# Score products of 128 query rows at a time in a cross-attention kernel with layer norm

## The chip, the cores and the metric

The kernel runs on one core of one Trainium2 chip. The metric is the device time of one execution in microseconds. Engines are named as in the profile: PE is the matmul engine and PEld its weight loads, DVE, ACT and POOL the vector, scalar and GpSimd engines, SP the engine that issues most of the DMAs.

## The reference, cut to what matters

Four batches of 2048 query rows of 512 numbers attend to 77 context rows each; there are 16 heads of 32 numbers. All data is float32. The result is added to the input and layer-normalised.

```
qs = (x @ wq) as 16 heads of 32          # x: (4, 2048, 512)
ks, vs = (ctx @ wk), (ctx @ wv)          # ctx: (4, 77, 512), as 16 heads of 32
scores = einsum('bhqd,bhkd->bhqk', qs, ks) / sqrt(32)
scores = where(mask, -inf, scores)       # (4, 16, 2048, 77)
attn   = einsum('bhqk,bhkd->bhqd', softmax(scores), vs)
out    = attn @ wo + x
result = (out - mean) / sqrt(var + 1e-5) * gamma + beta
```

## The kernel before

The 8192 query rows are 64 tiles of 128 rows. Query projections (`q_visit`, tiles `pq`) are made for groups of 512 rows; the output projection (`o_proj`, tiles `po`) and the scores are made by tile. Both projections run as three products of float32 parts split into a high and a low half (`wqh`/`wql`, `xth`/`xtl`, `woh`/`wol`, `AH`/`AL`), each with 128x128 weights. The scores and the products of attention with values (`av`, tiles `pa`) are plain float32 products.

`qd[t // 4]` holds the projected queries with the head dimension on the partitions: four heads stand one below the other, 32 partitions each, and `g` numbers the four such sets. `kct` holds the keys in the same way. So a score product `score(t, g, j, ...)` uses the 32 rows of the array at `HD * j`, has the queries of head `(g, j)` as its weights and streams the 77 columns of the keys. The four `j` use the four row groups of the array, and their results go to four PSUM banks (one bank per `j`, tiles `sc`), query rows on the partitions.

`scores` serves one tile. `scores_pair` and `scores_rest` serve two tiles `2b` and `2b + 1` together: 32 units of a head and a tile, eight for each `j`, six of them in the bank of their own (`sc_b_0` to `sc_b_3`) and two in a bank that two `j` share (`sc_b_e` and `sc_b_f`). For even `j` the units in the shared bank come first, for odd `j` last.

DVE then takes each head's scores with the mask and writes negated masked scores to `pbuf` and their minima to `nm` (`maxima`, one instruction for 128 rows of one head), ACT makes the exponentials and their sums (`exps`), DVE the reciprocals, POOL the division (`normalise`), DVE transposes in blocks (`transp`), SP's DMAs regroup the blocks into `PT`, and `av` multiplies by the values. ACT and DVE split the result into `AH` and `AL`; `o_proj`, the residual sum and the layer norm follow.

The order of all work is written by hand. Six tiles run in a loop of their own, with `scores`. Then `pair(n)` walks the words of `PAIR` for n = 3 to 26, two tiles each; a word such as `T1.30` is one step (`S` is `scores_pair`, `D` is `scores_rest`, `T` is `maxima`, `e` is `exps`, `Q` is `q_visit`, `O` is `o_proj`, `V` is `av`). `ORDER` then names the steps for the rest, with `S54` to `S63` as `scores` of one tile. On PE the sequence of a pair is: `av`, the scores of `S` and `D`, two output projections, two query projections.

Of the kernel before, what the change touches and what calls it, by code (L numbers as in the profile page):

```python
# [17 lines left out]
P = 128  # L18
# [8 lines left out]
GH = 4  # L27
# [49 lines left out]
def xattn_layernorm(  # L77
# [29 lines left out]
    def bank(name):  # L107
        while len(ring) % 8 in kept:
            ring.append(ring[-8])
        ring.append(ring[-8] if kept else ps.tile([P, 512], F32, tag="mm", name=name))  # L110
        return ring[-1]
# [49 lines left out]
    def keys_of(h):  # L161
        return slice(TAIL_K, NK2) if h % 2 == 0 else slice(0, NK)

    fx, gx, qd, qp, bat, pts = {}, {}, {}, {}, {}, {}
    scs, nmax, sums, bts, at, pas = {}, {}, {}, {}, {}, {}
# [142 lines left out]
    def scores(t):  # L308
        nmax[t] = sb.tile([P, H], F32, tag="nm", bufs=3, name=f"nm_{t}")
        sums[t] = sb.tile([P, H], F32, tag="sum", bufs=3, name=f"sum_{t}")  # L310
        sc = [bank(f"sc_{t}_{j}") for j in range(GH)]
        scs[t] = {(g, j): sc[j][:, g * NK : (g + 1) * NK] for g in range(NG) for j in range(GH)}
        for g in range(NG):
            for half in range(0, P, P // 2):
                for j in range(GH):
                    score(t, g, j, half, P // 2)

    def score(t, g, j, r0, n):
        q = slice(HD * j, HD * (j + 1))
        at = (t % 4) * P + r0  # L320
        nc.tensor.matmul(  # L321
            scs[t][g, j][r0 : r0 + n],
            qd[t // 4][q, g, at : at + n],
            kct[q, g, t // TPB, keys_of(j)],
            start=True,
            stop=True,
        )

    def scores_pair(b):
        for t in (2 * b, 2 * b + 1):  # L330
            nmax[t] = sb.tile([P, H], F32, tag="nm", bufs=3, name=f"nm_{t}")
            sums[t] = sb.tile([P, H], F32, tag="sum", bufs=3, name=f"sum_{t}")
            scs[t] = {}
        own = [bank(f"sc_{b}_{j}") for j in range(GH)]
        both = [bank(f"sc_{b}_{j}") for j in ("e", "f")]
        units = []
        for j in range(GH):
            mine = [(2 * b, g) for g in range(NG)] + [(2 * b + 1, g) for g in range(NG)]
            for i, (t, g) in enumerate(mine):
                bk, at = (own[j], i) if i < 6 else (both[j // 2], 2 * (j % 2) + i - 6)  # L340
                scs[t][g, j] = bk[:, at * NK : (at + 1) * NK]
            units.append(mine[6:] + mine[:6] if j % 2 == 0 else mine)
        for i in range(6):
            for half in range(0, P, P // 2):
                for j in range(GH):
                    score(*units[j][i], j, half, P // 2)
        held[b] = units

    def scores_rest(b):
        units = held.pop(b)  # L350
        for i in (6, 7):
            for js in ((0, 2), (3, 1)):
                for half in range(0, P, P // 2):
                    for j in js:
                        score(*units[j][i], j, half, P // 2)

    def maxima(t, lo, hi):
        pb = pbuf[t % NPB]
# [410 lines left out]
    for u in range(0, JOIN, 2):  # L769
        n = u // 2  # L770
# [5 lines left out]
        for t in (u - 4, u - 3):  # L776
            if t >= 0:
                load_x(t)
        scores(u)
        maxima(u, 0, H // 2)  # L780
        if u == 2:
# [53 lines left out]
        if u >= 4:  # L835
            av(n - 2)
            av_hi(n - 2, 0)
            av_hi(n - 2, 1)
        scores(u + 1)
        maxima(u + 1, 0, H // 4)  # L840
        if u >= 4:
# [42 lines left out]

    tile_ops = {
        "S": scores, "r": recip, "n": normalise, "t": transp, "W": av_tile, "x": load_x, "O": o_proj,
        "X": lambda t: resid(t, range(NC_D // 2 if t == NT - 1 else NC_D)), "+": residual, "u": rsqrt_one, "y": centre, "z": finish, "k": scale, "f": affine, "w": store,
        "v": bias_one, "K": stretch, "G": shift, "p": pool_scale, "I": act_mean, "J": act_squares, "M": keep,
# [48 lines left out]
    def pair(n):  # L937
        u = 2 * n
        words = PAIR.split()
        if n == JOIN // 2:  # L940
            words.remove("O-6")
            words.insert(words.index("D"), "O-6")
        for word in words:
            op, k, part, queue = read(word)
            if op == "S":
                scores_pair(n)
            elif op == "D":
                scores_rest(n)
            elif op in "LB":
                m, at = divmod(u, TPB)  # L950
                if m + 1 < NB and op == "L" and at == TPB - 10:
                    load_mask(m + 1)
                elif m + 1 < NB and op == "B" and at >= TPB - 8:
                    mask_quarter(m + 1, (at - TPB + 8) // 2)
            elif op == "P" and "." not in word:
                regroup(n + k)
            elif op in "Qq":
                if op == "Q" or divmod(2 * n + k, 4) in qp:
                    do(op, 2 * n + k)
            elif op in "gij":  # L960
                do(op, n + k)
            elif op in "PVab":
                if op in "PV" or n + k > JOIN // 2 - 3:
                    do(op, n + k, part, queue)
            elif u + k >= 0:
                do(op, u + k, part, queue)
# [54 lines left out]
```

## Time and profile before

| what | value |
|---|---|
| time, median of 3 runs | 506.53 us (506.32 to 507.22) |
| the profiled execution | 508.02 us, span 506.2 us |
| PE busy | 497.0 us, 98% of the span |
| ACT busy | 473.0 us, 93% |
| DVE busy | 463.0 us, 91% |
| POOL busy | 427.6 us, 84% |
| mean granted PE clock | 0.997 |

The times are of whole executions; the span is the time from the first to the last instruction of the profiled one. Rows of groups give line, engine, operation, output and inputs, the part of the array (rows*columns), shapes and count, then busy time and mean nanoseconds of one, then idle time before it and what ended it. In rows of a timeline the first number is the start and the second the length, both in microseconds. The chain that ended last is followed back from the last instruction, from each piece of work to what released it. A float32 product that is not split by the kernel shows in the trace as two weight loads and two matmuls.

### The profile page before, as it was taken

Reading aid. Unit: us, or ns where it says so; the run is one execution under the profiler, and the core shown is the slowest. Engines: PE = TensorE matmul, PEld = TensorE weight load, DVE = VectorE, ACT = ScalarE, POOL = GpSimd, SP = SyncE. Lnnn points to the kernel's source line nnn. Section 1 sums busy time; section 2 is a strip of 40 time slices with the busy share of each in tenths; the row PEclk is TensorE's granted clock in tenths of the full one; section 3 lists DMA queues with packets and bytes.
Section 4 is the critical chain, followed back from the end, with each engine's and each line's share of the span. In section 5 each row is a group of like instructions: output and inputs, shape, how many; then the busy total and the mean of one; then the engine's idle time right before and its main releaser. Section 6 shows DMA issues by size and latency. Waiting matters only on the chain.

```text
span 506.2 us, 20441 instructions
## 1 busy us (share of the span) xinstructions
PE 497.0 (98%) x6908; PEld 391.7 (77%) x6908; DVE 463.0 (91%) x2567; ACT 473.0 (93%) x2240; POOL 427.6 (84%) x384
## 2 busy tenths in 40 slices
PE   9999999999999999999999999999999999999995
PEld 7987678777777877777787777778777777777784
DVE  6698899999989988999998998999999889999997
ACT  6798899999999999999999999999999999999971
POOL 0559367989988988989998888999988888999995
PEclk9999999999999999999999999999999999999998
DMA  8945867677887778878777877877778787677665
GB/s 314 388 168 149 222 187 194 190 196 202 231 229 218 223 201 219 229 209 229 213 219 211 232 199 223 229 224 227 216 196 221 199 247 235 170 189 222 167 210 208
DMA packets 58280, 109.50 MB, mean 216 GB/s; under 512 B 9203, under 2 KB 10739, under 8 KB 58176
## 3 DMA queue, kind: packets, MB, share of 16 engines
q1 hardware_dynamic: 55776, 103.35, 71.7%
q0 software_dynamic: 1872, 4.20, 2.8%
q8 instruction: 55, 0.90, 0.8%
q10 hardware_dynamic: 528, 0.66, 0.4%
q14 instruction: 49, 0.40, 0.3%
HBM read 41.68 MB, written 16.78 MB: 115 GB/s over the span
## 4 chain that ended last, share of the span: by engine, by line
PE 79%; DVE 8%; ACT 7%; DMA 2%; issue 1%; SPq 1%; POOL 0%; POOLq 0%; DVEq 0%; ACTq 0%
PE pq L192 27%; PE po L564 26%; PE pa L459 10%; ACT pbuf L379 7%; PE sc L321 6%; DVE B L413 2%; PE sc L564 2%; DVE pbuf L364 2%; PE sc_e L321 2%; PE pk L218 1%; PE pq L725 1%; PE pq L190 1%; PE sc_f L321 1%; SPq L425 1%; DMA out<-o 1%
## 5 line engine op out<-in xcount | busy, mean ns | idle before, releaser
L379 ACT ACTIVATE pbuf<-pbuf,nm 128x77 f32<-128x77 f32 x1024 | 352.6, 349 | 8.6 <-DVE nm L364 7.8
L379 ACT ACTIVATION_READ_ACCUMULATOR pbuf<-pbuf,nm 128x1 f32 x1024 | 193.9, 189 | 0.0
L390 POOL TENSOR_TENSOR pbuf<-pbuf,ri 128x1232 f32<-128x1232 f32 x63 | 145.9, 2316 | 20.8 <-DVE ri L385 17.4
L364 DVE CUSTOM_DVE_ANT_0 pbuf<-sc,mb 128x77 f32<-128x77 f32 x828 | 143.9, 231 | 6.9 <-PE sc L321 6.4
L192 PE MATMUL pq<-xtl,wqh 128*128 128x512 f32 (+1 forms) x256 | 98.3, 384 | 0.0
L192 PE MATMUL pq<-xth,wql 128*128 128x512 f32 (+1 forms) x256 | 98.2, 384 | 0.0
L413 DVE STREAM_TRANSPOSE B<-pbuf 128x1280 f32<-128x1280 f32 x63 | 94.6, 1503 | 0.4
L564 PE MATMUL po<-woh,AH 128*128 128x512 f32 x224 | 90.7, 405 | 0.0
L192 PE MATMUL pq<-xth,wqh 128*128 128x512 f32 (+1 forms) x230 | 88.6, 385 | 0.0
L564 PE MATMUL po<-wol,AH 128*128 128x512 f32 x224 | 87.3, 390 | 0.0
L592 POOL TENSOR_TENSOR o<-o,gam 128x512 f32<-128x512 f32 x53 | 68.7, 1295 | 21.5 <-ACT o L588 21.5
L564 PE MATMUL po<-woh,AL 128*128 128x512 f32 x224 | 86.5, 391 | 0.0
L364 DVE DVE_READ_ACCUMULATOR2_ANT nm<- 128x1 f32 x1024 | 84.4, 82 | 0.0
L593 POOL TENSOR_TENSOR o<-o,bet 128x512 f32<-128x512 f32 x53 | 68.3, 1289 | 4.2
L180 POOL TENSOR_TENSOR xtl<-xtf,xth 128x1024 fp32r<-128x1024 f32 x28 | 67.4, 2409 | 0.1
L459 PE MATMUL pa<-PT,vsb 96*32 96x256 f32 x960 | 58.2, 382 | 1.6 <-DVE vsb L267 1.0
L321 PE MATMUL sc<-kct,q 32*64 32x77 f32 x3312 | 56.0, 238 | 0.5 <-DVE q L209 0.5
L192 PEld LDWEIGHTS pq<-xth,wql 128*128 128x128 f32 x256 | 48.2, 188 | 8.4
L192 PEld LDWEIGHTS pq<-xtl,wqh 128*128 128x128 f32 x256 | 48.1, 188 | 8.4
L321 PEld LDWEIGHTS sc<-kct,q 32*64 32x64 f32 x3312 | 49.3, 130 | 6.5 <-issue 4.4
L564 PEld LDWEIGHTS po<-woh,AH 128*128 128x128 f32 x224 | 42.0, 188 | 10.7 <-DVE nm L364 0.4
L192 PEld LDWEIGHTS pq<-xth,wqh 128*128 128x128 f32 x230 | 43.2, 188 | 9.0
(191 smaller groups left out, 855.1 us busy)
## 6 DMA issues: line engine op xcount, KB each, us to landing
PT<-B SPq DMA_DIRECT2D x355, 128.0 KB
xtf<-xT SPq DMA_DIRECT2D x28, 512.0 KB
o<-x SPq DMA_DIRECT2D x56, 256.0 KB
out<-o SPq DMA_DIRECT2D x56, 256.0 KB
PT<-B POOLq DMA_DIRECT2D x16, 128.0 KB, 4.5
o_end<-x SPq DMA_DIRECT2D x7, 256.0 KB
out<-o_end SPq DMA_DIRECT2D x7, 256.0 KB
xtf<-xT SPq DMA_DIRECT2D x4, 256.0 KB
```

The costliest lines, as they stand in the source:

```text
L180: nc.gpsimd.tensor_tensor(l, fx.pop((g, c)), h.bitcast(F32), ALU.subtract)
L190: nc.tensor.matmul(pq[:, cols], wc, r[:, c, cols], start=False, stop=False)
L192: nc.tensor.matmul(pq, wc, r[:, c, rs], start=(n == 0), stop=(n == 11))
L321: nc.tensor.matmul(scs[t][g, j][r0 : r0 + n], qd[t // 4][q, g, at : at + n], kct[q, g, t // TPB, keys_of(j)], start=True, stop=True,)
L364: nc.vector.tensor_tensor_reduce(pb[:, i // 2, (i % 2) * NK : (i % 2 + 1) * NK], scs[t][g, j], mb[:, t % TPB, keys_of(h)], -1.0, CEIL, ALU ...
L379: nc.scalar.activation(p, p, AF.Exp, bias=nmax[t][:, i : i + 1], scale=-1.0, accum_out=sums[t][:, i : i + 1])
L390: nc.gpsimd.tensor_tensor(pv, pv, rv.to_broadcast((P, NP, 2, NK)), ALU.mult)
L413: nc.vector.transpose(bt.rearrange("p c q r -> p q c r"), pbuf[t % NPB].rearrange("p q (c r) -> p q c r", c=5),)
L459: nc.tensor.matmul(pas[b, g // 2][HD * j : HD * (j + 1), (g % 2) * BLK : (g % 2 + 1) * BLK], vsb[:, 2 * b // TPB, HD * h : HD * (h + 1)], ...
L564: nc.tensor.matmul(pos[t], a[:, c, rs], w[:, c], start=(first and n == 0), stop=(n == 11))
L592: nc.gpsimd.tensor_tensor(o, o, gam, ALU.mult)
L593: nc.gpsimd.tensor_tensor(o, o, bet, ALU.add)
```

## The change

A score product takes all 128 query rows of its tile as weights, so it uses 32 rows and all 128 columns of the array, where it took 64 rows of the tile and 64 columns. One product replaces two. Nothing else is edited; the banks, the heads' order and the hand-written order stay as they are.

```diff
         for g in range(NG):
-            for half in range(0, P, P // 2):
-                for j in range(GH):
-                    score(t, g, j, half, P // 2)
-
-    def score(t, g, j, r0, n):
+            for j in range(GH):
+                score(t, g, j)
+
+    def score(t, g, j):
         q = slice(HD * j, HD * (j + 1))
-        at = (t % 4) * P + r0
+        at = (t % 4) * P
         nc.tensor.matmul(
-            scs[t][g, j][r0 : r0 + n],
-            qd[t // 4][q, g, at : at + n],
+            scs[t][g, j],
+            qd[t // 4][q, g, at : at + P],
             kct[q, g, t // TPB, keys_of(j)],
...
         for i in range(6):
-            for half in range(0, P, P // 2):
-                for j in range(GH):
-                    score(*units[j][i], j, half, P // 2)
+            for j in range(GH):
+                score(*units[j][i], j)
...
         for i in (6, 7):
             for js in ((0, 2), (3, 1)):
-                for half in range(0, P, P // 2):
-                    for j in js:
-                        score(*units[j][i], j, half, P // 2)
+                for j in js:
+                    score(*units[j][i], j)
```

On PE, the start of a pair's scores (n = 4; `sc_e`, `sc_1`, `sc_f` and `sc_3` are the banks of `j` = 0 to 3 there). Before, the first two units of each `j`:

```order
L321 MATMUL sc_e<-kct,q_907 64x77 [waits DVE_49,PE_49]
L321 MATMUL sc_1_1335<-kct,q_907 64x77 [waits DVE_49]
L321 MATMUL sc_f<-kct,q_907 64x77 [waits DVE_49]
L321 MATMUL sc_3_1337<-kct,q_907 64x77 [waits DVE_49,PE_49]
L321 MATMUL sc_e<-kct,q_907 64x77
L321 MATMUL sc_1_1335<-kct,q_907 64x77
L321 MATMUL sc_f<-kct,q_907 64x77
L321 MATMUL sc_3_1337<-kct,q_907 64x77
L321 MATMUL sc_e<-kct,q_907 64x77 [waits DVE_49]
```

and now:

```order
L320 MATMUL sc_e<-kct,q_827 128x77 [waits DVE_49]
L320 MATMUL sc_1_1207<-kct,q_827 128x77 [waits DVE_49]
L320 MATMUL sc_f<-kct,q_827 128x77 [waits DVE_49]
L320 MATMUL sc_3_1209<-kct,q_827 128x77 [waits DVE_49]
L320 MATMUL sc_e<-kct,q_827 128x77 [waits DVE_49]
```

The second round of four (the other 64 rows) is gone, and the second unit follows the first directly. The end of the same pair's scores, before:

```order
L321 MATMUL sc_0_1334<-kct,q_907 64x77
L321 MATMUL sc_2_1336<-kct,q_907 64x77
L321 MATMUL sc_0_1334<-kct,q_907 64x77
L321 MATMUL sc_2_1336<-kct,q_907 64x77
L321 MATMUL sc_f<-kct,q_907 64x77
L321 MATMUL sc_e<-kct,q_907 64x77
L321 MATMUL sc_f<-kct,q_907 64x77
L321 MATMUL sc_e<-kct,q_907 64x77
L564 MATMUL po_1433<-woh,AH_1324 128x512 [waits DVE_49]
```

and now:

```order
L320 MATMUL sc_0_1206<-kct,q_827 128x77
L320 MATMUL sc_2_1208<-kct,q_827 128x77
L320 MATMUL sc_f<-kct,q_827 128x77
L320 MATMUL sc_e<-kct,q_827 128x77
L561 MATMUL po_1273<-woh,AH_1196 128x512 [waits DVE_49]
```

Four products stand before the first output projection where eight stood; the projection itself has not moved. The rows of DVE, ACT, POOL and SP are the same in number and order.

## Prediction

> **What bounds the kernel now.** I read the page's busy table first, then the chain that ended last in order of time, then stretches, then single instructions of a score burst.
>
> ```profile
> PE 497.0 (98%) x6908; PEld 391.7 (77%) x6908; DVE 463.0 (91%) x2567; ACT 473.0 (93%) x2240; POOL 427.6 (84%) x384
> ```
>
> PE is busy for 98%, but the busy time of a pipelined engine proves little, so the chain that ended last comes next (start, length, what):
>
> ```profile
> 92.84 5.66 PE po L564 x24
> ...
> 201.66 1.36 PE pq L192 x6
> 203.25 3.88 PE pq L192 x17
> 207.13 1.86 PE pa L459 x32
> 209.44 0.94 PE sc L321 x46
> 210.69 5.68 PE po L564 x24
> ...
> 402.15 5.67 PE po L564 x24
> ```
>
> From 92.84 to 402.15 us the chain never leaves PE: output projections (po), the next group's query projections (pq), attention times values (pa), a score burst (sc), and po again. There are 21 periods between the first and the last row, so a period of two tiles is 309.31 / 21 = 14.729 us, and whatever the score burst gains or loses the period gains or loses. The code has 16 attention-value products in a pair and the row counts 32: each fp32 product runs as two passes, each with a weight load and a matmul record. So the 64 score products of a pair are 128 passes.
>
> ```profile
> 90.00:415.00 325.00, 325.00 (x4622) 254.46 (x4614) 301.89 (x1730) 319.65 (x1520) 293.79 (x243) 1.00 0.79 217
> 415.00:465.00 50.00, 49.56 (x855) 38.18 (x851) 49.09 (x318) 49.74 (x267) 47.34 (x43) 1.00 0.75 207
> ```
>
> These stretches (busy us of PE, PEld, DVE, ACT, POOL; then the granted clock, 1.00) show how near the others are: ACT is busy for 319.65 of 325 us, so if PE became faster, ACT would soon be the bound. If PE becomes slower, all of them merely wait more. In the last stretch ACT (49.74 of 50) and DVE (49.09) are as full as PE.
>
> **One burst.** The timeline of PE around the burst at 194.29, one of the shortest:
>
> ```profile
> 194.29 0.28 PE L321 MATMUL sc_e<-kct,q 32*64 32x77 f32 x1
> ...
> 194.41 0.23 PE L321 MATMUL sc_e<-kct,q 32*64 32x77 f32 x1
> ...
> 194.48 0.23 PE L321 MATMUL sc_e<-kct,q 32*64 32x77 f32 x1
> ...
> 194.55 0.23 PE L321 MATMUL sc_e<-kct,q 32*64 32x77 f32 x1
> ...
> 195.76 0.23 PE L321 MATMUL sc_e<-kct,q 32*64 32x77 f32 x1
> 195.92 0.50 PE L564 MATMUL po<-woh,AH 128*128 128x512 f32 x1
> 196.26 0.39 PE L564 MATMUL po<-wol,AH 128*128 128x512 f32 x1
> ```
>
> Eight passes (four row groups, two halves of the columns) start close together, and then a set of eight every 0.07 us (194.41, 194.48, 194.55; read to the nanosecond 0.067, which I use). Only the first set shows its weight load: 0.28 against 0.23 us, so a 64-column load costs 0.05 us when nothing hides it, and the first po matmul, 0.50 against 0.39, shows 0.11 us for 128 columns. So now load (0.05) is shorter than stream (0.067), the streams are the limit, and a clean burst would be 16 sets x 0.067. The burst is longer than that: it takes 195.92 - 194.29 = 1.63 us, since its middle, which I leave out, runs in less even order. An average burst follows from the period and the fixed rest, 208.93 - 195.92 = 13.01 us:
>
> ```profile
> 208.93 0.28 PE L321 MATMUL sc_e<-kct,q 32*64 32x77 f32 x1
> ...
> 210.62 0.50 PE L564 MATMUL po<-woh,AH 128*128 128x512 f32 x1
> ```
>
> 14.729 - 13.01 = 1.715 us per burst on average; this one has 1.69. A burst of one tile (64 passes), as it stands in the first six and the last ten tiles, takes 419.78 - 418.90 = 0.88 us:
>
> ```profile
> 418.90 0.32 PE L321 MATMUL sc<-kct,q 32*64 32x77 f32 x8
> ...
> 419.78 0.50 PE L192 MATMUL pq<-xth,wqh 128*128 128x512 f32 x1
> ```
>
> **The change, part by part.** It issues 1024 score products instead of 2048, so 2048 passes instead of 4096. Each streams the same 77 columns of keys, so a pass still streams for 0.067 us, and a set is now four passes, one on each row group. The number of sets is the same: 16 in a pair, 8 in a tile. Half of the instructions saves nothing while the stream of a set is what ends last. What changes is the load: 128 columns of queries into each row group instead of 64 into each of two tiles.
>
> ```profile
> L321 PEld LDWEIGHTS sc<-kct,q 32*64 32x64 f32 x3312 | 49.3, 130 | 6.5 <-issue 4.4 <-DVE nm L364 0.8 <-DVE q L209 0.6
> ...
> L564 PEld LDWEIGHTS po<-woh,AH 128*128 128x128 f32 x224 | 42.0, 188 | 10.7 <-DVE nm L364 0.4
> ...
> L459 PEld LDWEIGHTS pa<-PT,vsb 96*32 96x32 f32 x960 | 29.0, 109 | 26.1 <-issue 5.1 <-DVE q L209 3.9 <-PE pq L192 1.4
> ```
>
> The mean of a load (the number behind the bar and the busy time) goes with its columns, whatever the rows: 109 ns at 32 (96 rows), 130 at 64 (32 rows), 188 at 128 (128 rows), that is 0.7 to 0.9 ns a column upon some 80 to 90 ns. From 64 to 128 columns this adds 58 ns, as the exposed 0.05 and 0.11 us do. No row shows a 32x128 load. Near the end, 128-column loads follow each other with matmuls that stream only 128 columns in one pass; their spacing shows what they cost (the loads, then one of the matmuls):
>
> ```profile
> 498.10 0.19 PEld L544 LDWEIGHTS sc<-ident,xtl 128*128 128x128 f32 x1
> 498.21 0.19 PEld L544 LDWEIGHTS sc<-ident,xth 128*128 128x128 f32 x1
> 498.32 0.19 PEld L544 LDWEIGHTS sc<-ident,xtl 128*128 128x128 f32 x1
> ```
>
> ```profile
> 498.16 0.28 PE L544 MATMUL sc<-ident,xtl 128*128 128x128 f32 x1
> ```
>
> 0.11 us each; starts read to the nanosecond give 0.112. The stream of 128 columns, a quarter of a po matmul's 512 (5.67 / 24 = 0.236 us each), is 0.06 and not the limit. I take 0.112 for a set of the changed burst, because this is the row with the same columns and a stream shorter than the load. Below, the bound is 0.067 (the load would hide entirely); above, load and stream one after the other, 0.11 + 0.067 = 0.18.
>
> The new pair burst: exposed first load 0.11, fifteen further sets 15 x 0.112 = 1.68, 0.02 until the fourth tile of the last set starts, and 0.155 from the last score matmul to po, as now (195.92 - 195.76): 1.965 us against 1.715, so +0.25. Point of balance: 1.715 = 0.285 + 15 s gives s = 0.095 us; above that step the change loses. The uneven middle, some 0.45 us of the 1.715 (a clean burst would take 0.05 + 15 x 0.067 + 0.05 + 0.155 = 1.26), I cost at nothing in the new burst: half as many instructions have a longer time to be issued in, and what paces each set is the load.
>
> [...]
>
> The sum. Twenty-two steady pair bursts: 22 x 0.25 = 5.5 us. Sixteen bursts of one tile: 0.11 + 7 x 0.112 + 0.02 + 0.155 = 1.07 against 0.88, +0.19 each, 3.0 us; two irregular pair bursts before 80 us, +0.25 each, 0.5 us. Of these 3.5 us not all reaches the end: PE itself waits once in the front, and towards the end ACT and DVE are full and work on scores that came earlier.
>
> ```profile
> PE pa L459 <- DVE vsb L267: 1.0, 1, 1.0
> ```
>
> ```profile
> DVE pbuf L364 <- PE sc_f L321: 19.9, 22, 1.2
> ```
>
> I take six tenths, 2.1 us, with 0 and 3.5 as ends. The second row is DVE's wait for each burst, 22 times 0.9 us: it grows with the burst; DVE has 23 of 325 us free in the long stretch (301.89 busy), and a period that is longer by the same 0.25 gives it back. Total 5.5 + 2.1 = +7.6 us. The profiled execution took 508.02 us around a span of 506.2; that would be 515.6 and 513.8. It lies 1.5 above the median of the three runs (506.53), so I forecast 506.53 + 7.6 = **514.1 us**.
>
> **The rivals.** *Loads stay hidden, the change gains.* If a row group of 32 takes its 128 columns within the 0.067 us of the stream, a pair burst is 0.285 + 15 x 0.067 = 1.29 us (0.285 is the first load, the fourth tile and the end, 0.11 + 0.02 + 0.155), 0.42 less. Then ACT bounds: it has 5.35 us left in 325, so some 0.24 us a period, 5.3 us in all, and about 1 us from the ends: 500 us. For it speaks that eight loads now run side by side at 0.067 us a set, so the path into the array is wide; against it, that the same load is twice as long in every row with 128 columns. It needs a step under 0.095. Chance 0.08.
>
> [...] Chance 0.04.
>
> *Loads don't overlap streams.* If a tile's next load waits for its stream, a set takes 0.18 and a pair 0.02 + 0.155 + 16 x 0.18 = 3.05, +1.34 x 22 = 29 us, and with six tenths of 16 x 0.73 + 2.7 near 545 us. Against it: the 24 po matmuls with 512 columns take 5.67 us, 0.236 each, which leaves no room for a separate 0.11 us of load. Chance 0.03.
>
> [...]
>
> **How the numbers follow.** Forecast 0.85, rivals 0.08, 0.04 and 0.03. Within the forecast: 0.107 a set takes 2 us off; the ends passing nothing or everything, 2.1 off or 1.4 on; an uneven middle of 0.15 us a burst, 3.3 on. That makes 509.5 to 518.5; both ends outside hold about 0.2. A measurement of this kernel tells about 0.2% (1 us) from no change. Faster 0.08, same 0.05, slower 0.87.
>
> **What the new profile should show.** Score loads as 32x128 at a mean near 188 ns, 2048 score passes; within a burst, a set of four every 0.11 us; 1.96 us from the first score matmul to po; a period of 14.98; DVE's wait for the burst near 1.1 us; ACT less full. Sets at 0.067 with ACT closing up would prove me wrong on the load; sets at 0.112 with a total under 510 would prove me wrong on the path.

## The result, and the profile after

The changed kernel takes 515.09 us (median of 4 runs, 514.77 to 515.32) against 506.54: a ratio of 1.0166, 95% interval 1.0153 to 1.0178, or 8.55 us slower. The forecast was 514.1. The profiled execution took 514.77 us around a span of 513.0.

The page's busy table and the first lines of its chain:

```profile
PE 505.7 (99%) x4860; PEld 400.2 (78%) x4860; DVE 461.9 (90%) x2567; ACT 475.4 (93%) x2240; POOL 427.5 (83%) x384
...
PE 95%; DVE 2%; DMA 1%; ACT 1%; issue 1%; POOL 0%; POOLq 0%
```

PE has 2048 fewer loads and matmuls (4860 instead of 6908) and is busy for 8.7 us more. In the page of before, the chain's line reads:

```profile
PE 79%; DVE 8%; ACT 7%; DMA 2%; issue 1%; SPq 1%; POOL 0%; POOLq 0%; DVEq 0%; ACTq 0%
```

Before, the chain left PE at the front and again between 415 and 463 us; now it stays on PE there too. The chain in order of time:

```profile
93.89 5.67 PE po L561 x24
99.56 1.36 PE pq L192 x6
101.15 3.88 PE pq L192 x17
105.03 1.86 PE pa L456 x32
107.50 0.99 PE sc L320 x34
108.85 5.67 PE po L561 x24
...
408.05 5.67 PE po L561 x24
```

The pieces of 5.67, 1.36, 3.88 and 1.86 us are those of before to within 0.02 us; only the score burst has changed. The period is (408.05 - 93.89) / 21 = 14.960 us instead of 14.729. One burst on the timeline of PE:

```profile
196.58 0.33 PE L320 MATMUL sc_e<-kct,q 32*128 32x77 f32 x1
...
196.75 0.27 PE L320 MATMUL sc_e<-kct,q 32*128 32x77 f32 x1
...
196.87 0.27 PE L320 MATMUL sc_e<-kct,q 32*128 32x77 f32 x1
...
196.98 0.27 PE L320 MATMUL sc_e<-kct,q 32*128 32x77 f32 x1
...
198.34 0.27 PE L320 MATMUL sc_f<-kct,q 32*128 32x77 f32 x1
198.54 0.50 PE L561 MATMUL po<-woh,AH 128*128 128x512 f32 x1
```

Sets of four follow each other every 0.11 to 0.12 us, where sets of eight came every 0.067. The weight loads show the pace directly: the first loads into one of the four tiles now, and then the first loads for `sc_e` before:

```profile
196.58 0.18 PEld L320 LDWEIGHTS sc_e<-kct,q 32*128 32x128 f32 x1 [0.41 <-issue]
...
196.69 0.18 PEld L320 LDWEIGHTS sc_e<-kct,q 32*128 32x128 f32 x1
...
196.80 0.19 PEld L320 LDWEIGHTS sc_e<-kct,q 32*128 32x128 f32 x1
```

```profile
194.29 0.13 PEld L321 LDWEIGHTS sc_e<-kct,q 32*64 32x64 f32 x1 [0.41 <-issue]
...
194.32 0.13 PEld L321 LDWEIGHTS sc_e<-kct,q 32*64 32x64 f32 x1
...
194.35 0.13 PEld L321 LDWEIGHTS sc_e<-kct,q 32*64 32x64 f32 x1
```

Now each row group starts a load every 0.11 us. Before, one started every 0.03 us, so the two 64-column loads of a row group fitted in 0.06 us, little more than the 0.05 us that one costs where nothing hides it. Every score matmul behind the first set now lasts 0.27 us, not 0.23, and the last one starts 0.20 us before `po`, not 0.155. This reads as a matmul that starts when its tile is free and then waits some 0.05 us for its own weights; as the ends of matmuls in the trace are modelled, it is a reading and not a measurement.

The burst takes 198.54 - 196.58 = 1.96 us (1.954 read to the nanosecond, in all 22 steady bursts). A burst of one tile takes 426.05 - 424.99 = 1.06:

```profile
424.99 0.35 PE L320 MATMUL sc<-kct,q 32*128 32x77 f32 x4
...
426.05 0.50 PE L192 MATMUL pq<-xth,wqh 128*128 128x512 f32 x1
```

The load itself, in the table of groups, and the stretch and the wait that answer to those of before:

```profile
L320 PEld LDWEIGHTS sc<-kct,q 32*128 32x128 f32 x1656 | 60.8, 186 | 6.0 <-issue 4.2 <-DVE ri L382 0.7 <-DVE mvt L605 0.7
```

```profile
90.00:415.00 325.00, 325.00 (x3173) 256.33 (x3173) 296.55 (x1713) 316.36 (x1494) 289.36 (x239) 1.00 0.78 212
```

```profile
DVE pbuf L361 <- PE sc_f L320: 25.9, 22, 1.3
```

A 32x128 load has a mean of 186 ns, as the 128x128 loads have 188. ACT is busy for 316.36 of 325 us (319.65 before), DVE for 296.55 (301.89), with fewer instructions in the window (1494 instead of 1520 on ACT), and DVE's wait for a burst has gone from 0.9 to 1.2 us: the others wait more for PE.

### The profile page after: what moved, and what is told of

Read it like the earlier page. It is cut to its first block, busy times and chain, and to the rows that moved or that the text cites. A ratio compares the mean times of both kernels' runs of the same rounds, so it can differ in the third digit from the quotient of the medians.

```text
span 513.0 us, 16216 instructions
## 1 busy us (share of the span) xinstructions
PE 505.7 (99%) x4860; PEld 400.2 (78%) x4860; DVE 461.9 (90%) x2567; ACT 475.4 (93%) x2240; POOL 427.5 (83%) x384
## 4 chain that ended last, share of the span: by engine, by line
PE 95%; DVE 2%; DMA 1%; ACT 1%; issue 1%; POOL 0%; POOLq 0%
PE pq L192 32%; PE po L561 31%; PE pa L456 11%; PE sc L320 10%; PE sc_e L320 3%; PE sc L561 2%; PE pv L258 2%; PE pk L218 1%; PE pq L722 1%; PE pq L190 1%; DMA xtf<-xT 1%; DVE st L599 0%; DVE o_end L564 0%; DVE AL L509 0%; ACT AH L505 0%
## 5 line engine op out<-in xcount | busy, mean ns | idle before, releaser
L320 PE MATMUL sc<-kct,q 32*128 32x77 f32 x1656 | 67.0, 274 | 0.0
L320 PEld LDWEIGHTS sc<-kct,q 32*128 32x128 f32 x1656 | 60.8, 186 | 6.0 <-issue 4.2
```

The lines of the kernel that those rows point to most:

```text
L320: nc.tensor.matmul(scs[t][g, j], qd[t // 4][q, g, at : at + P], kct[q, g, t // TPB, keys_of(j)], start=True, stop=True,)
```

## The experiments

Theory A is the prediction's: the load of 128 columns paces a set. B is its rival, that a pass is slower in a 128-column tile for another reason. Theory C is on the kernel before: what made its 64-row bursts uneven is the supply of products to PE.

**Longer streams in both kernels.** The key tile has 96 columns, 19 of them a second copy. Each product streams all of them into its bank, in an order in which the extra columns are overwritten by the next product.

```diff
-            scs[t][g, j],
+            wide[t, g, j],              # the same place, 19 columns wider
             qd[t // 4][q, g, at : at + P],
-            kct[q, g, t // TPB, keys_of(j)],
+            kct[q, g, t // TPB, :],
```

In the changed kernel:

> The changed kernel (32x128 tiles), but every score product streams all 96 columns of the key tile instead of 77; the 19 extra columns land where later products overwrite them, so the scores read are the same. Theory A (the load of 128 columns paces a set, 0.112 us): the stream grows from 0.067 to about 0.083 us and stays under the load, so sets stay at 0.112, a pair burst at 1.95 to 1.97 us, the time at 515 to 516 us. Rival B (the pass itself is slower in a 128-column tile, so 0.112 is a stream time): sets grow by 96/77 to 0.14, a pair burst by 0.42 us, the time to about 526 us.

Measured: 516.16 us, ratio to the kernel before 1.0181 (1.0162 to 1.0201). In the kernel before, with the same edit:

> The kernel before (32x64 tiles) with the same 96-column streams. Theory A: here the stream paces the packed sets, so they go from 0.067 to 0.083 us; if that held for all 16 sets of a pair the burst would grow by 0.25 us and the time reach some 513 us; where the issue of products and not the stream sets the uneven middle, the growth is smaller, about 0.1 us a pair, 509 us. Rival B says the same of this kernel (a set is a stream), so it is the comparison with the 128-column run that tells the two apart: under A the extra columns cost here and not there.

Measured: 511.22 us, ratio 1.0080 (1.0062 to 1.0098), between the two times named. The timelines of PE, first with 128 columns of weights, then with 64:

```profile
196.83 0.34 PE L328 MATMUL sc_e<-kct,q 32*128 32x96 f32 x1
...
197.02 0.27 PE L328 MATMUL sc_e<-kct,q 32*128 32x96 f32 x1
...
197.13 0.27 PE L328 MATMUL sc_e<-kct,q 32*128 32x96 f32 x1
...
198.80 0.50 PE L571 MATMUL po<-woh,AH 128*128 128x512 f32 x1
```

```profile
194.71 0.24 PE L329 MATMUL sc_e<-kct,q 32*64 32x96 f32 x1
...
194.80 0.24 PE L329 MATMUL sc_e<-kct,q 32*64 32x96 f32 x1
...
194.88 0.24 PE L329 MATMUL sc_e<-kct,q 32*64 32x96 f32 x1
...
420.64 1.05 PE L329 MATMUL sc<-kct,q 32*64 32x96 f32 x64
421.62 0.50 PE L192 MATMUL pq<-xth,wqh 128*128 128x512 f32 x1
```

With 128 columns, sets stay at 0.11 us and the burst at 1.97: a quarter more streaming is hidden under the load, all but some 0.016 us at the end of the burst. With 64, sets go from 0.067 to 0.08 us and the burst of one tile from 0.88 to 0.98. B is excluded by the first run, in which sets of 0.14 and 526 us should have come. The pair bursts with 64 columns grew by less than the stream alone would have them: the period is 14.81, 0.08 us longer and not 0.25, so their uneven middle is not paced by the stream.

**Fewer columns to load.** The changed kernel with 96 query rows in a product; DVE, ACT and POOL work on 96 partitions, so their instructions stay as many and as long in the free dimension (an exponential takes 349 ns on average against 347, one of `maxima` 227 against 231), and the scores of 32 rows of each tile are left out. The three `pbuf` are cleared whole at the start.

```diff
-            scs[t][g, j],
-            qd[t // 4][q, g, at : at + P],
+            scs[t][g, j][:ROWS],            # ROWS = 96
+            qd[t // 4][q, g, at : at + ROWS],
```

> The changed kernel with 96 instead of 128 query rows in each score product; the scores, exponentials and sums of the other 32 rows of a tile are left out, all instructions are as many as in the changed kernel. Theory A (load columns pace a set): 96 columns load in 0.080 us and a set takes about 0.085, so a pair burst is 0.08 + 15 x 0.085 + 0.02 + 0.155 = 1.53 us (1.95 with 128 rows), a burst of one tile 0.85; the period falls to 14.53, where ACT's work of 14.5 a period begins to bound; time 504 to 508 us. Rival B (a pass in a 128-column tile takes 0.112 whatever it loads): 1.95 us, 515 us.

Measured: 503.79 us, ratio 0.9942 (0.9927 to 0.9957), below the kernel before and just below the 504 to 508 us expected. No run shows the 0.080 us that went into this forecast for a load of 96 columns; an estimate from the 0.112 us of 128 columns is 0.084, and what the timeline shows is the time of a set:

```profile
192.45 0.30 PE L321 MATMUL sc_e<-kct,q 32*96 32x77 f32 x1
...
192.60 0.24 PE L321 MATMUL sc_e<-kct,q 32*96 32x77 f32 x1
...
192.68 0.24 PE L321 MATMUL sc_e<-kct,q 32*96 32x77 f32 x1
...
193.98 0.50 PE L562 MATMUL po<-woh,AH 128*128 128x512 f32 x1
```

```profile
L321 PEld LDWEIGHTS sc<-kct,q 32*96 32x96 f32 x1656 | 48.4, 160 | 6.6 <-issue 4.1 <-DVE q L210 1.1 <-DVE nm L362 0.4
```

The same number of products, the same streams, the same issue, 32 columns fewer in each load: sets of 0.08 to 0.09 us and a burst of 193.98 - 192.45 = 1.53 us, as theory A has it to the second digit. Fifteen of the 22 steady bursts take that long; the other seven take 1.65 to 1.79 us, so the period is 14.60 us and not 14.53. What holds these seven up is not settled. The step lies under the point of balance (0.095 us), and the kernel is faster than before, but it leaves work out. These runs can't tell the load from another cost that grows with the columns of weights. For the load speaks that a set of 128 columns (0.112 us) takes as long as a load of 128 columns that nothing hides (0.11 us, in the first `po` matmul). The control of the run with 96 rows:

> Control for the run with 96 rows: the same code with all 128 rows, that is the changed kernel with only POOL's clearing of three buffers at the start made larger. All theories: as the changed kernel, 515 us within 1 us, pair burst 1.954.

Measured: 514.64 us (1.0157, 1.0140 to 1.0174), the changed kernel's time within half a microsecond; the larger clearing costs nothing that can be seen.

**The two halves of the change.** The 128-row form in `scores` alone, for the first six and last ten tiles, and then in `scores_pair` and `scores_rest` alone:

> Half of the change: the bursts of one tile (the first six and last ten tiles) use 128 rows, the bursts of two tiles stay at 64. Theory A with the path as predicted: sixteen bursts grow from 0.88 to 1.06 us, and a part of those 2.9 us reaches the end, 507.5 to 509.5 us. If all of the change's cost lay in the steady pairs: 506.5 us.

> The other half: bursts of two tiles at 128 rows, bursts of one tile at 64. Theory A: 22 steady bursts at 1.954 instead of 1.715 us, +5.3 us, and two irregular ones with up to +0.5: 511.5 to 512.5 us, period 14.96 us. The two halves together should give the 8.55 us of the whole change.

Measured: 510.07 us (1.0059, 1.0041 to 1.0076) and 513.63 (1.0129, 1.0112 to 1.0145), that is +2.9 and +6.4 us against the 507.2 of the kernel before beside them. The absolute times lie 0.6 and 1.1 us above what was expected; about 0.7 of each is that the kernel before ran at 507.2 there. In the second run the period is 14.96 us, as expected. The sum, 9.3 us, covers the whole change's 8.55 within the intervals.

The first run's +2.9 us is what sixteen bursts longer by 0.18 us would give if all of it reached the end, but its profile doesn't bear that out. Against the profile of before, the front (up to the `po` at 93.33) is 0.5 us longer and the end (from the `po` at 403.80) 0.9 us; the other 1.2 us lie in the steady stretch between, whose code is that of before. There the chain has one stop that the profile puts down to nothing:

```profile
123.84 1.02 issue
```

The bursts themselves grew by less, too. In the trace of before, the last ten bursts of one tile include four that take 1.03 to 1.24 us until PE's next matmul, not 0.88, and now take 1.06. So the sixteen grew by 2.0 us in sum, and how much of it reaches the end can't be read from this run.

**The middle of the 64-row bursts.** Four products of 32 rows instead of two of 64 (`P // 4` for `P // 2` in all three loops):

> The kernel before with 32 query rows a product (32x32 tiles, 4096 products, 8192 passes). [...] Theory C (the uneven middle of the 64-row bursts is the supply of products: about 16 products, 32 passes, go in each 0.37 us): a pair has 128 products, eight such windows, so the burst takes 2.8 to 3.1 us instead of 1.7 and the time goes to 530 to 545 us. Rival D (only load and stream count, and the middle has another cause): the burst stays at 1.2 to 1.7 us and the time at 500 to 507 us.

Measured: 625.18 us, ratio 1.233 (1.225 to 1.240). Rival D is out, and theory C was far too low. What fits it is the shortest case, a burst of one tile (five of the sixteen take this long), which now has 64 products, as a pair had with 64 rows, and half of a pair's streams:

```profile
523.64 0.28 PE L321 MATMUL sc<-kct,q 32*32 32x77 f32 x6
...
525.13 0.50 PE L192 MATMUL pq<-xth,wqh 128*128 128x512 f32 x1
```

```profile
PEld sc L321 <- issue: 57.6, 40, 3.0
```

It takes 525.13 - 523.64 = 1.49 us, close to the 1.63 of a short pair burst before, though eight sets at the 0.067 us of the kernel before would stream for 0.53 us in all. That fits a limit by the number of products, some 0.023 us each (1.49 / 64); one comparison doesn't show it. The pair bursts, 4.8 us on average, have stalls besides, up to 3.0 us in which the loads wait for nothing that the profile shows, 57.6 us in sum; what these are is not settled.

**Mixing the widths.** If supply limits 64-row products and the load 128-row ones, a mix could beat both. First, two whole rounds of a pair at 128 rows:

```diff
-            for half in range(0, P, P // 2):
+            rows = P if i in (2, 5) else P // 2
+            for r0 in range(0, P, rows):
                 for j in range(GH):
-                    score(*units[j][i], j, half, P // 2)
+                    score(*units[j][i], j, r0, rows)
```

> The kernel before, but in a pair burst two of the eight rounds (the third and the sixth) use 128 rows: 56 products instead of 64 in a pair. Theory C (supply of products limits 64-row bursts, load limits 128-row ones): the mix costs the rows' loads and streams 6 x 0.133 + 2 x 0.224 = 1.25 us and the supply 56 / 16 x 0.37 = 1.30 us, so the burst falls from 1.715 to about 1.5 us and the time to about 502 us, if the array changes tile width at no cost. Rival E (each change of width drains the array, some 0.09 us or more, four times a burst): the burst is 1.8 to 2.0 us and the time 509 to 514 us.

Measured: 517.30 us, ratio 1.0201 (1.0171 to 1.0231). On the timeline of PE the burst goes from 196.62 to 198.76:

```profile
196.62 0.28 PE L321 MATMUL sc_e<-kct,q 32*64 32x77 f32 x1
...
198.76 0.50 PE L565 MATMUL po<-woh,AH 128*128 128x512 f32 x1
```

2.14 us, somewhat over even rival E, whose 0.09 us is an estimate from the end of a burst before (0.155 us from the last score matmul to `po`, less a stream of 0.067); that the array drains at a change of width is not shown. Loads and streams account for 1.25 and the two ends for some 0.25, which leaves 0.64 for four changes of width: an estimate of 0.16 us each. The timeline, read to the nanosecond, agrees. From the last set of 64 columns before a 128-row round to the second one behind it there go 0.71 us; at the steps of 0.067 and 0.112 it would be 0.36, so each of the two changes costs 0.18. The other 64-row sets of this burst come at an even 0.067 us, so no uneven middle hides in the 0.64. Second, one row group at 128 and three at 64 in each of six rounds:

```diff
                 for j in range(GH):
-                    score(*units[j][i], j, half, P // 2)
+                    if (i + j) % 4:
+                        score(*units[j][i], j, half, P // 2)
+                    elif half == 0:
+                        score(*units[j][i], j, 0, P)
```

> As the run before, but in each of the first six rounds one of the four row groups (another one each time) uses 128 rows and the other three 64, 58 products in a pair. With no cost for a change of width (C): supply 58 / 16 x 0.37 = 1.34 us, burst about 1.5 us, 502 us. If widths can't stand side by side in the array (E): twelve changes a burst at 0.09 us or more, a burst of 2.8 us or more, over 525 us.

Measured: 612.14 us in the profiled execution, at a mean granted clock of 0.93, and 624.62 to 635.21 us in three others, at 0.89 to 0.91. Even the shortest is 1.208 times the 506.86 us of the kernel before. The time of rival E, over 525 us, came; that widths can't stand side by side in the array, its reason, is not shown. From the chain of its profile, then the long stretch and the first and third of these output projections as stretches of their own:

```profile
333.98 7.18 PE po L567 x24
354.49 7.21 PE po L567 x24
373.68 5.67 PE po L567 x24
```

```profile
90.00:415.00 325.00, 325.00 (x3345) 249.12 (x3344) 233.59 (x1337) 249.37 (x1176) 224.84 (x187) 0.91 0.62 168
333.98:341.16 7.18, 7.18 (x26) 5.83 (x26) 6.43 (x53) 6.80 (x41) 1.68 (x2) 0.78 0.25 77
373.68:379.35 5.67, 5.67 (x25) 4.70 (x26) 5.67 (x47) 5.29 (x31) 3.06 (x3) 1.00 0.51 189
```

The bursts grew to between 4.6 and 6.0 us, and the granted clock fell to 0.91 in the long stretch. Where it was 0.78, two output projections took 7.18 us; where it was 1.00, they took 5.67. None of the complete kernels tried beats the kernel before.

## Why the prediction was right

- *PE is the bound.* Right. Every piece of the period but the burst kept its length, and the chain ran on PE for 95%.
- *A load of 128 columns on 32 rows takes as long as one on 128 rows, 0.112 us a set.* Right, and shown: 186 ns against 188 for one, bursts of 1.96 and 1.06 us where 1.965 and 1.07 were worked out. The runs with 96-column streams and with 96 rows tell load from stream: more streaming costs next to nothing while the load is longer, fewer columns to load make the set shorter, also below the point of balance.
- *The streams set the pace before.* Right for the packed sets (0.067 to 0.083 us with longer streams) and for the first half of a burst of one tile, which takes 0.88 us in all where eight clean sets would make 0.72. The average pair burst was slower than its streams by the uneven middle, as the prediction had it.
- *The middle costs nothing afterwards.* Right: the burst has no part beyond its sets. Its cause, the supply of products, was only argued there; the runs with 32 rows and with longer streams fit it without showing it, the first with stalls that stay unexplained.
- *Steady bursts, 22 x 0.25 = 5.5 us.* The period grew by 0.231 us, so 5.1 us; the burst is 1.954 us and not 1.965, and the rest of the period 13.006 and not 13.01.
- *The ends, 2.1 of 3.5 us.* Both factors were off, in opposite directions. The 3.5 us were too many: between the two traces the sixteen bursts of one tile grew by 2.0 us in sum and not by 3.0, and the two irregular pair bursts by 0.2 and not by 0.5. The share of six tenths was too small: the two profiled spans differ by 6.8 us; less 5.1, the ends gave 1.7 of these 2.2 us. The argument for a share below one was that ACT and DVE are full in the last stretch and have earlier scores to work on; the chain, which had passed through them there, now stays on PE, so most of a later burst reached the end. By the medians the ends gave twice as much, 8.55 - 5.1 = 3.4 us, because the profiled execution of before lay 1.5 us above its median. In which stretch it lost that can't be seen, so what the ends really gave stays open between 1.7 and 3.4 us.
- *The total, +7.6 us.* Measured +8.55. By the medians the steady bursts were put 0.4 us too high and the ends 1.3 too low. That the sum came within 1 us is owed to the step of a set, which carries most of it and was right, and in the ends partly to luck.
- *DVE's wait near 1.1, ACT less full.* 1.2 us, and 316.36 of 325.

Of the rivals, that of hidden loads needed a step under 0.095 us and the runs gave 0.11; that of serial loads would have made a set 0.18, where the trace has a set every 0.11 us, so a row group loads while it streams. The chance of 0.04 stood for a time as before, 506.5 us; it is 515.09. No row and no run shows the 0.107 us a set that the range of the forecast allows for; in the steady bursts a set came every 0.112 us.

## What to carry to other kernels

For float32 products with little to stream, compare the load of a tile with the stream of one pass (here 0.067 us for 77 columns, 0.87 ns a column against 0.46 in `po`); here 64 columns load in 0.05 us under a stream of 0.067, and 128 load in 0.11 and pace everything. Here two half-width tiles on the same rows took their pair of loads in 0.06 us, where the full-width tile took 0.11 for its one, so halving the instructions by widening the tile can cost time although the array does the same work. The point of balance can be worked out beforehand from one burst and one row of loads.

## What the runs showed of the hardware that was not expected

- A change between 64-column and 128-column tiles in the middle of a burst cost an estimated 0.16 to 0.18 us, and four of them more than the mix could gain here.
- In the two runs with frequent changes of width or very small tiles, the granted clock of PE fell: to 0.91 in the long stretch with one wide row group in each round, with PE busy for all of its 325 us, and to 0.95 with 32x32 tiles, against 1.00 before. Two output projections took 7.18 us at 0.78 instead of 5.67 at 1.00. What brings the clock down there was not tested.
- With 32x32 tiles, the shortest bursts took 0.023 us for each product, and pair bursts stalled for up to 3.0 us on nothing that the profile names.
